# An early place for one set of expert weights, and edge gathers paced by ScalarE, in a graph layer with a routed FFN

## The chip, the cores and the metric

The kernel runs on 1 core of one Trainium2 chip. A core has TensorE (PE, with its weight loads shown apart as PEld), VectorE (DVE), ScalarE (ACT), GpSimd (POOL) and SyncE (SP), each with its own queue of instructions, and 16 DMA engines that all of them share. POOL also issues the indirect DMAs (gathers and scatters by a list of rows). The metric is the time of one execution on the device in microseconds (us); lower is better.

## The reference

Everything is float32. There are N = 6250 nodes of D = 256 features, 100000 edges sorted by their destination, 8 heads, and 8 experts. In outline:

```python
x = x + gnn(layernorm(x), edges, ...)     # graph attention, then a dense FFN
x = x + moe(layernorm(x), ...)            # router, top 2 of 8 experts, FFN of each

# gnn
xn = layer_norm(x, ln1_g, ln1_b)
h = (xn @ W).reshape(N, 8, 32)
e = leaky_relu(a_src[src] + a_dst[dst])           # loops i -> i are added to the edges
alpha = softmax of e over the edges of each dst
agg = segment_sum(h[src] * alpha, dst)
out = layer_norm(agg + xn @ W_res + bias, ln2_g, ln2_b)
return out + gelu_tanh(out @ ffn_w1 + ffn_b1) @ ffn_w2 + ffn_b2     # 256 -> 1024 -> 256

# moe
probs = softmax(x @ Wr + br); top 2, weights scaled to sum 1
y_e = gelu(xe_e @ W1[e] + b1[e]) @ W2[e] + b2[e]                    # 256 -> 1024 -> 256
return sum over the two chosen experts of weight * y_e
```

## The kernel before

The nodes lie in 49 tiles of 128 rows. A first stage (up to about 117 us) makes the tables: `tab_s` in HBM holds each node's `h` and its attention factors, `xt_d` the turned normed input, and the sums `acc_lo` and `acc_hi` in SBUF start with the loops' share.

Then one planned loop (`while s < NG + LASTST ...`, under `tc.manual_schedule()`) writes out the order of all instructions by steps s. It mixes four kinds of work.

- **Edge steps.** There are 196. Step s fetches 512 edges (`fetch`, L865): four gathers of 128 rows of `tab_s` into one `gs` buffer; there are four such buffers. The later stages of an edge step stand in later steps: `spread` (s), `turn_spread` (s+1), `give` (s+2), `weigh` (s+3, DVE: L905 and L909, which frees `gs`), `add_tiles` (s+4, PE L924), and, where a group of steps ends, `add_nodes` (s+5: PE L949, ACT L952 into `added`) and `sum_up` (s+6, DVE L961). There are 110 groups. Edges are taken from the last destinations to the first.
- **Residual products** (`first_unit`, 25 units of two tiles): load of `xt_d` into `xtf`, product with `wres` (L1225), eviction into `rg`, store to `res_d`.
- **Node units** (`node_unit`, 25): when all edges into two tiles are summed, DVE divides and normalises (`divide`, `norm_out`), ACT applies it (`norm_rows`), the dense FFN runs (`net`: `turn` L1025, eight `up` L1042 with eviction to `ht` L1046, `down` L1055), DVE adds up (`add_out`, `take_up`, `norm_new`), and PE makes the router's logits (L1197). Every two units, `chunk_tasks` ranks the tokens (`mark`, `count`, `rank`), makes the list of blocks that are now complete (`enlist`), and scatters the normed rows into `xs` (POOL, L1458), sorted by expert. After the list of the next to last chunk, `clear` (L1474) writes zeros behind each expert's rows, eight DMAs of 390 KB; scatters that stand behind the clears wait until these have landed.
- **Expert blocks** (`block_loads`, `block_unit`; 53 on these inputs): 256 rows of one expert (a few have 128). SP loads W1 and W2 of the expert (1 MB each) and the rows `xb` (L1529); DVE notes the destinations (L1551); then the same `net`; DVE adds the bias (L1561), ACT scales (L1567), and POOL gives the rows back to the output with an adding indirect DMA, two per block (L1571). A block's rows are loaded once the scatters of the chunk that completes it have landed.

Each queue works in order. A step has room for so much work of each engine (`ROOM`: PE 7.5 us, less 1.3 for the edges; POOL one operation besides the gathers). Tasks wait in `pending`, in the order in which they were made, and go into a step when the tasks they need stand in an earlier one; a new unit or block is made only while the queued PE work is under `QUEUE` = 40 us. The last node unit is `urgent`: its tasks go in front.

**Places in SBUF.** `acc_hi` is freed when node tile KHI has been divided (around step 64); only then does the pool `moew` open there, with two sets of expert weights, and only if the pool `first` of the residual products (`wres`, two `xtf`, two `rg`) is closed. A third set (`moew3`) comes when the edges are over. So no expert block stands in the first third of the edge steps.

Of the kernel before, what the change touches and what calls it, by code (L numbers as in the profile page):

```python
# [223 lines left out]
def gnn_moe_kernel(  # L224
# [613 lines left out]
    first_ = ctx.enter_context(ExitStack())  # L838
    fp = first_.enter_context(tc.tile_pool(name="first", bufs=2, side="right"))
    wres = fp.tile([P, KD, D], F32, name="wres", bufs=1)  # L840
# [11 lines left out]

    def step_tiles(s, a):

        q, i = order[s]
        t0, m = groups[q]
        return a[:, t0:t0 + G * m].rearrange("p (j m) -> p j m", m=m)[:, :, i]

    def fetch(s):
        gs = bg.tile([P, G, DT], F32, name="gs")  # L860
        q, i = order[s]
        t0, m = groups[q]
        for j in range(G):
            t = t0 + j * m + i
            nc.gpsimd.indirect_dma_start(  # L865
                out=gs[:, j, :], out_offset=None, in_=tab_s,
                in_offset=bass.IndirectOffsetOnAxis(ap=srce[:, t:t + 1], axis=0))
        live[s, "gs"] = gs
# [16 lines left out]
    def turn_spread(s):  # L885
        po = cps.tile([P, KD, 2 * P], F32, name="pt", bufs=2)
        nc.tensor.transpose(po[:, 0, :P], live[s, "oh"].rearrange("p j r -> p (j r)"), ident)  # L887
        oht = bw.tile([P, P], F32, name="oht")
        nc.scalar.activation(oht, po[:, 0, :P], AF.Copy)
        live[s, "oht"] = oht  # L890

    def give(s):

        pz = bps.tile([P, P], F32, name="pz")[:, :G * 2 * H]
        nc.tensor.matmul(pz, live.pop((s, "oht")), live[order[s][0], "qd"].rearrange(  # L895
            "p j c -> p (j c)"), start=True, stop=True)
        fac = bw.tile([P, G * 2 * H], F32, name="fac")
        nc.scalar.activation(fac, pz, AF.Copy)  # L898
        live[s, "pz"] = fac
# [15 lines left out]
    def add_tiles(s):  # L915

        q, i = order[s]
        last = i == groups[q][1] - 1
        oh, msg = live.pop((s, "oh")), live.pop((s, "msg"))
        if i == 0:  # L920
            live[q, "pl"] = bps.tile([P, DA], F32, name="pl")
        pl = live[q, "pl"]
        for j in range(G):
            nc.tensor.matmul(pl[j * W32:(j + 1) * W32, :], oh[:, j, :], msg[:, j, :],  # L924
                             start=i == 0, stop=last)
        if last:
            part = bw.tile([P, DA], F32, name="part")
            nc.scalar.activation(part, pl, AF.Copy)
            live[q, "part"] = part
# [16 lines left out]
    def add_nodes(q):  # L946
# [3 lines left out]
        added = bw.tile([P, 2, DA], F32, name="added")  # L950
        for b in range(2):
            nc.scalar.activation(added[:, b, :], p2, AF.Copy, scale=here[:, b, q:q + 1])  # L952
# [66 lines left out]
    def turn(src, to, env, scale=None):  # L1019
# [8 lines left out]
        if scale is None:  # L1028
            nc.scalar.activation(xt[:, :, :n * P], pt[:, :, :n * P], AF.Copy)
        else:  # L1030
            for k in range(KD):
                nc.scalar.activation(xt[:, k, :n * P], pt[:, k, :n * P], AF.Identity,  # L1032
                                     bias=scale[:, KD + k:KD + k + 1], scale=scale[:, k:k + 1])
        env[to] = xt

    def up(c, env, w1, func, b):
# [7 lines left out]
        for e in range(c - 1, c + 1) if c % 2 else ():  # L1044
            ht = cw.tile([P, 2 * P], F32, name="ht", bufs=2 * KF)
            nc.scalar.activation(ht[:, :W], ph[:, e % 2, :W], func, bias=b[:, e:e + 1], scale=1.0)  # L1046
            env["ht", e] = ht
# [10 lines left out]
    turns, downs_, ups_ = [], [], []  # L1058
# [3 lines left out]
    def net(env, src, deps, w1, w2, func, b, more=(), scale=None, more2=()):  # L1062
# [5 lines left out]
        ups = [task(lambda c=c: up(c, env, w1(), func, b()), "PE", 0.46 * n, [tn, *more, *free])  # L1068
# [17 lines left out]
        downs_.append(dn[-1])  # L1086
        return dn[-1]
# [49 lines left out]
    def norm_rows(n, env):  # L1137
        for j in range(n):
            oj = env["res"][:, j, :]
            nc.scalar.activation(oj, oj, AF.Identity, bias=env["nm"][:, j:j + 1],  # L1140
                                 scale=env["r"][:, j:j + 1])

    def add_out(n, env):

        o = cw.tile([P, 2, D], F32, name="o", bufs=1)
        nc.vector.tensor_tensor(o[:, :n], env["res"][:, :n],
# [37 lines left out]
    def make_normed(n, env, u):  # L1184
# [3 lines left out]
        for j in range(n):  # L1188
            nc.scalar.activation(xe[:, j, :], env["xin"][:, j, :], AF.Identity,
                                 bias=env["nb"][:, j:j + 1], scale=env["rs"][:, j:j + 1])  # L1190
        env["xe"] = xe

    def logits(n, env):
# [6 lines left out]
        nc.scalar.activation(lt[:, :n * E], pl[:, :n * E], AF.Copy)  # L1200
# [13 lines left out]
    def load_first(t0, n, env):  # L1214
        xt = fp.tile([P, 2, KD, P], F32, name="xtf")
# [13 lines left out]
    def take_product(n, env):  # L1229
        rg = fp.tile([P, 2, D], F32, name="rg")  # L1230
        nc.scalar.activation(rg[:, :n], env["py"][:, :n], AF.Copy)
# [6 lines left out]
    firsts, first_loads = [], []  # L1238

    def first_unit(u):  # L1240
        t0, n, _ = units[u]
        env = {}
        first_loads.append(task(lambda: load_first(t0, n, env), "SP", 0.0,
                                [(d, 0) for d in back(firsts, 2)]))
        pr = task(lambda: first_product(n, env), "PE", 0.95 * n, [(first_loads[-1], 2)], take="py")
        ab = task(lambda: take_product(n, env), "ACT", 0.3 * n,
                  [pr, *[(d, 0) for d in back(firsts, 2)]], free="py")
# [12 lines left out]
    def node_unit(u, env):  # L1260
# [4 lines left out]
        ao = task(lambda: add_out(n, env), "DVE", 0.7 * n, [nr])  # L1265
        dn = net(env, lambda: env["res"], [nr], lambda: w1_sb, lambda: w2_sb,
                 AF.Gelu_apprx_tanh, lambda: prm[:, PR_FB1:PR_FB1 + KF],
                 scale=lambda: prm[:, PR_L2G:PR_L2G + 2 * KD])
        tk = task(lambda: take_up(t0, n, env), "DVE", 0.35 * n, [dn, ao], free="py")
# [60 lines left out]
    def weight(t0, n, env):  # L1330

        nc.scalar.activation(env["less"][:, :n], env["less"][:, :n], AF.Exp)
# [12 lines left out]
    def count(env):  # L1345
# [5 lines left out]
        nc.scalar.activation(rt.rearrange("p a e -> p (a e)"), pr[:, :8 * E], AF.Copy)  # L1351
        env["pr"] = rt

    def rank(t0, n, env):
# [19 lines left out]
        nc.vector.tensor_add(cnt, cnt, incl[:, :, 3])  # L1374

    def enlist(lo, hi, final, begun):
# [32 lines left out]
        if final:  # L1409
# [14 lines left out]
        is_ = cw.tile([P, n * m * E], F32, name="is_", bufs=1).rearrange(  # L1424
            "p (n e) -> p n e", n=n)
        ge = cw.tile([P, n * m * E], F32, name="ge", bufs=1).rearrange(
            "p (n e) -> p n e", n=n)
# [7 lines left out]
        red = cw.tile([P, n], F32, name="redb", bufs=1)  # L1435
# [129 lines left out]
    def weigh_block(env):  # L1565
        for j in range(env["n"]):
            nc.scalar.activation(env["yb"][:, j, :], env["yb"][:, j, :], AF.Copy,  # L1567
                                 scale=env["wt"][:, j:j + 1])
# [11 lines left out]
    def block_loads(i):  # L1580
# [5 lines left out]
        env["pool"] = 1 if len(moew) > 1 and 1 not in pools[-2:] else 0  # L1586
        user = [j for j in range(i) if pools[j] == env["pool"]][-2 + env["pool"]:][:1]
        if env["pool"] == 0 and pools.count(0) < 2:
            user = []
# [48 lines left out]
    with tc.manual_schedule():  # L1638
        nc.sync.dma_start(xs[E * CAP:, :].rearrange("(p r) d -> p r d", r=2),
                          blank[:, None, :].to_broadcast([P, 2, DX]))  # L1640
        while s < NG + LASTST or pending or u < len(units) or len(blocks) < NS:
# [13 lines left out]
            if len(firsts) == len(units) and firsts[-1].step is not None and fp:  # L1655
                first_.close()
                fp = None
            if last_hi and last_hi[0].step is not None and not moew and not fp:
                hi_pool.close()
                moew.append(ctx.enter_context(tc.tile_pool(name="moew", bufs=2, side="right")))  # L1660
            nb = len(blocks) + len(ahead)
            if moew and len(ahead) < 1 + len(moew) and nb < NS and any(n > turn_of[nb]
# [3 lines left out]
            while sum(t.cost for t in pending if t.eng == "PE") < QUEUE:  # L1666
                if (u < len(units) and units[u][2] <= s - LASTST
                        and not (ahead and was_nodes)):
# [15 lines left out]
                elif ahead:  # L1684
# [10 lines left out]
            run_tasks(s, room)  # L1695
            s += 1
# [43 lines left out]
```

## Time and profile before

| | us |
|---|---|
| three runs, median (lowest to highest) | 1735.18 (1732.95 to 1740.66) |
| the profiled execution, its own time | 1738.49 |
| its span, first to last instruction | 1736.7 |
| first gather of the edges starts | 117.5 |
| first product of an expert block starts | 549.7 |
| last gather starts | 1450.2 |
| last product with the dense FFN weights (L1055) starts | 1529.5 |

Mean granted TensorE clock: 0.96 of full speed. DMA moved 334.91 MB.

A group line names line, engine and operation, tile written and tiles read, count; then busy us and the mean ns of one; then the idle time ahead of them and what ended it. In a timeline a row begins with the start and the length, and the bracket at its end has the idle time before it and who released it; rows of the same kind are merged (x4). float32 products are recorded as two matmuls each, and records of neighbours overlap, so that the pace is read from starts and not from the length of one. A wait is put down to what came last.

### The profile page before, as it was taken

To read this page: it belongs to the slowest core of one execution; us is meant where nothing else is said; L and a number is where in the kernel's file an instruction comes from. 1 tells how busy PE (TensorE), PEld (TensorE's weight loads), DVE (VectorE), ACT (ScalarE), POOL (GpSimd) and SP (SyncE) were. 2 spreads that over 40 slices of the span, in tenths; PEclk is the share of its full clock that TensorE was granted. 3 is DMA by queue.
4 is the path that set the end of the run, shared out by engine and by line. 5 is a ranking of instruction groups with operands and counts; after the bars stand their busy time and mean duration, and the time that the engine had idled before them with its cause. 6 is when DMAs were issued, how large, how long until landed. Compare 5 with 4: busy or idle time off the path is not lost.

```text
span 1736.7 us, 28706 instructions
## 1 busy us (share of the span) xinstructions
PE 1555.9 (90%) x8577; PEld 1253.7 (72%) x8577; DVE 982.9 (57%) x3512; ACT 803.7 (46%) x2063; POOL 1155.2 (67%) x1190
## 2 busy tenths in 40 slices
PE   5866898989977999999999999998988998899996
PEld 3643676767656878788888887786866876788885
DVE  6855788888888765766666554337434335131000
ACT  4843454544535554555555444444433433343332
POOL 4437776777777777777778778777777774412222
PEclk9987899999988999999999999999999999999998
DMA  6886564566446667586676676776577766847672
GB/s 199 264 214 203 175 188 141 160 175 164 140 135 219 210 197 211 159 241 167 210 219 195 182 228 199 228 200 208 176 211 211 234 188 196 264 115 233 191 222 41
DMA packets 232898, 334.91 MB, mean 193 GB/s; under 512 B 45169, under 2 KB 189082, under 8 KB 232734
## 3 DMA queue, kind: packets, MB, share of 16 engines
q1 hardware_dynamic: 170892, 190.31, 34.1%
q0 software_dynamic: 58944, 139.58, 30.4%
q10 hardware_dynamic: 2898, 3.09, 0.6%
q8 instruction: 71, 1.16, 0.3%
q14 instruction: 93, 0.76, 0.1%
HBM read 275.95 MB, written 61.10 MB: 194 GB/s over the span
## 4 chain that ended last, share of the span: by engine, by line
PE 48%; DMA 8%; POOL 7%; issue 6%; DVE 5%; ACT 2%; SPq 1%; DVEq 0%; POOLq 0%; ACTq 0%
PE py L1055 20%; PE ph L1042 19%; DMA gs<-tab_s,srce 6%; POOL gs L865 5%; PE pl L924 3%; PE pt L949 1%; PE pt L1025 1%; PE pt L887 1%; DMA out_dram<-yb,tos 1%; ACT turned_in L1032 1%; POOL out_dram L1571 1%; DVE msg L909 1%; PE pz L895 1%; POOL xs L1458 1%; PE ph L1197 1%
## 5 line engine op out<-in xcount | busy, mean ns | idle before, releaser
L865 POOL DMA_INDIRECT gs<-tab_s,srce x784 | 823.3, 1050 | 252.8 <-issue 198.3
L1042 PE MATMUL ph<-turned_in,w1b 128*128 128x256 f32 (+1 forms) x1696 | 422.1, 379 | 8.8 <-ACT turned_in L1032 7.7
L1055 PE MATMUL py<-w2b,ht 128*128 128x256 f32 x1648 | 418.3, 383 | 3.3 <-DMA w2b<-in_L_ffn_W_dram 2.9
L1042 PEld LDWEIGHTS ph<-turned_in,w1b 128*128 128x128 f32 x1696 | 318.7, 194 | 55.2 <-ACT turned_in L1032 12.0
L1055 PEld LDWEIGHTS py<-w2b,ht 128*128 128x128 f32 x1648 | 313.4, 193 | 45.4 <-issue 3.7
L1046 ACT ACTIVATE ht<-ph,pc 128x256 f32<-128x256 f32 (+1 forms) x424 | 175.2, 465 | 363.7 <-PE ph L1042 363.4
L1571 POOL DMA_INDIRECT out_dram<-yb,tos x103 | 166.1, 1613 | 193.4 <-ACT yb L1567 131.7
L909 DVE TENSOR_TENSOR msg<-gs,msg 128x1024 f32<-128x1024 f32 x196 | 240.5, 1227 | 7.0 <-DVE msg L908 0.4
L924 PE MATMUL pl<-msg,oh 128*32 128x264 f32 x1568 | 134.1, 415 | 86.9 <-DVE msg L909 86.5
L905 DVE TENSOR_TENSOR ww<-gs,fac 128x64 f32<-128x64 f32 x196 | 43.8, 224 | 277.9 <-DMA gs<-tab_s,srce 239.2
L1042 PE MATMUL ph<-turned_in,w_sb 128*128 128x256 f32 (+1 forms) x800 | 193.7, 382 | 6.0 <-ACT ht L1046 5.1
L1055 PE MATMUL py<-w_sb,ht 128*128 128x256 f32 x784 | 190.2, 380 | 0.0
L1042 PEld LDWEIGHTS ph<-turned_in,w_sb 128*128 128x128 f32 x800 | 150.1, 194 | 27.6 <-ACT ht L1046 6.5
L1055 PEld LDWEIGHTS py<-w_sb,ht 128*128 128x128 f32 x784 | 144.5, 190 | 25.0 <-issue 3.5
L1458 POOL DMA_INDIRECT xs<-xe,slot x98 | 107.5, 1096 | 55.8 <-issue 41.2
L1046 ACT ACTIVATE ht<-ph,prm 128x256 f32<-128x256 f32 (+1 forms) x200 | 82.6, 467 | 121.5 <-PE ph L1042 121.4
L898 ACT ACTIVATE fac<-pz 128x64 f32<-128x64 f32 x196 | 44.0, 225 | 188.5 <-PE pz L895 105.1
L1561 DVE TENSOR_TENSOR yb<-py,b2b 128x512 f32<-128x512 f32 (+1 forms) x53 | 35.7, 673 | 153.6 <-PE py L1055 153.6
L924 PEld LDWEIGHTS pl<-msg,oh 128*32 128x32 f32 x1568 | 32.1, 110 | 102.8 <-issue 54.4
L952 ACT ACTIVATE added<-pt,here 128x264 f32<-128x264 f32 x220 | 93.8, 478 | 20.1 <-PE pt L949 13.0
L887 PEld LDWEIGHTS pt<-ident,oh 128*128 128x128 f32 x196 | 28.3, 144 | 95.9 <-issue 42.0
L961 DVE TENSOR_TENSOR acc_lo<-acc_lo,added 128x528 f32 x56 | 39.6, 708 | 92.7 <-ACT added L952 79.6
(359 smaller groups left out, 2038.1 us busy)
## 6 DMA issues: line engine op xcount, KB each, us to landing
w1b<-in_L_ffn_W_dram SPq DMA_DIRECT2D x53, 1024.0 KB
w2b<-in_L_ffn_W_dram SPq DMA_DIRECT2D x53, 1024.0 KB
xb<-xs SPq DMA_DIRECT2D x50, 260.0 KB
gs<-tab_s,srce POOLq DMA_INDIRECT x784
b2b<-in_L_ffn_b_dram SPq DMA_DIRECT2D x53, 128.0 KB
tab_s<-hg SPq DMA_DIRECT2D x12, 544.0 KB
xt_d<-xt SPq DMA_DIRECT2D x12, 512.0 KB
xtf<-xt_d SPq DMA_DIRECT2D x24, 256.0 KB
```

The source lines that it names most:

```text
L865: nc.gpsimd.indirect_dma_start(out=gs[:, j, :], out_offset=None, in_=tab_s, in_offset=bass.IndirectOffsetOnAxis(ap=srce[:, t:t + 1], axis=0))
L887: nc.tensor.transpose(po[:, 0, :P], live[s, "oh"].rearrange("p j r -> p (j r)"), ident)
L898: nc.scalar.activation(fac, pz, AF.Copy)
L905: nc.vector.tensor_tensor(ww, gs[:, :, D:], live.pop((s, "pz")).rearrange("p (j c) -> p j c", j=G), op=ALU.mult)
L909: nc.vector.tensor_tensor(msg[:, :, :D].rearrange("p t (h d) -> p t h d", h=H), gs[:, :, :D].rearrange("p t (h d) -> p t h d", h=H), msg[: ...
L924: nc.tensor.matmul(pl[j * W32:(j + 1) * W32, :], oh[:, j, :], msg[:, j, :], start=i == 0, stop=last)
L952: nc.scalar.activation(added[:, b, :], p2, AF.Copy, scale=here[:, b, q:q + 1])
L1042: nc.tensor.matmul(ph[:, c % 2, :W], w1[:, k, c * P:(c + 1) * P], env["in"][:, k, :W], start=k == 0, stop=k == KD - 1)
L1046: nc.scalar.activation(ht[:, :W], ph[:, e % 2, :W], func, bias=b[:, e:e + 1], scale=1.0)
L1055: nc.tensor.matmul(env["py"][:, j, :], env["ht", c][:, j * P:(j + 1) * P], w2[:, c, :], start=c == 0 and "row" not in env, stop=c == KF - 1)
L1458: st = nc.gpsimd.indirect_dma_start(out=xs, out_offset=bass.IndirectOffsetOnAxis(ap=slots[k][:n, t:t + 1], axis=0), in_=xes[u // 2][:n, pl ...
L1571: st = nc.gpsimd.indirect_dma_start(out=out, out_offset=bass.IndirectOffsetOnAxis(ap=tos[:, b, j:j + 1], axis=0), in_=env["yb"][:, j, :], ...
```

## The change

1. **A place for one weight set beside the edges.** The pool `first` goes. A pool `moew1` (`ew0`), opened ahead of the edges, holds one set (W1, W2). Until the residual products are through, its W2 space holds `wres` and three `rg`, its W1 space four `xtf`; so loads of the residual inputs run four units ahead and not two. Once the last residual unit is stored, the set serves the expert blocks. `moew2` (one set) opens when `acc_hi` is free, `moew3` after the edges, as before: three sets in the end as before, but the first one earlier. While there is one set, a block unit is made only when its weights and rows are on their way, and nodes and blocks needn't take turns. A block takes the set that was used longest ago.
2. **Space for it**: `added` has one buffer and not two; `ht` 12 and not 16, with dependencies that keep the ups behind the downs that free their buffers; `add_out` multiplies in place in `res` and therefore stands behind the turn that reads `res`; the tiles of `enlist` are sized once.
3. **Gathers behind ScalarE.** All of ScalarE's operations of a step are noted (`act`). The second, third and fourth gather of step s wait for the operation at one, two and three quarters of step s-1's list, if that has at least eight.

```diff
-    first_ = ctx.enter_context(ExitStack())
-    fp = first_.enter_context(tc.tile_pool(name="first", bufs=2, side="right"))
-    wres = fp.tile([P, KD, D], F32, name="wres", bufs=1)
+    ew0 = gnn.enter_context(tc.tile_pool(name="moew1", bufs=1))
+    early = ew0.tile([P, KD, F], F32, name="w1b").rearrange("p k (i c) -> p (k i) c", c=2 * D)
+    early2 = ew0.tile([P, KF, D], F32, name="w2b")
+    wres = early2[:, :KD, :]
+    early = [early[:, i, :] for i in range(4)] + [
+        early2[:, i * KD:(i + 1) * KD, :].rearrange("p k d -> p (k d)") for i in range(1, 4)]
...
+    acts = [[]]
+    def act(*a, **k):
+        i = nc.scalar.activation(*a, **k)
+        acts[-1].append(i.ins)
+        return i
...
+        ahead_ = acts[-2] if len(acts) > 1 else []
         for j in range(G):
             t = t0 + j * m + i
-            nc.gpsimd.indirect_dma_start(
+            ld = nc.gpsimd.indirect_dma_start(
                 out=gs[:, j, :], out_offset=None, in_=tab_s,
                 in_offset=bass.IndirectOffsetOnAxis(ap=srce[:, t:t + 1], axis=0))
+            if j and len(ahead_) >= 2 * G:
+                tc.add_manual_dep(ld.ins, ahead_[len(ahead_) * j // G].name, ...)
...
-        added = bw.tile([P, 2, DA], F32, name="added")
+        added = bw.tile([P, 2, DA], F32, name="added", bufs=1)
...
-            ht = cw.tile([P, 2 * P], F32, name="ht", bufs=2 * KF)
+            ht = cw.tile([P, 2 * P], F32, name="ht", bufs=3 * KF // 2)
...
+        last = dns[-1][-KF // 2:] if dns else []
+        ups = [task(lambda c=c: up(c, env, w1(), func, b()), "PE", 0.46 * n,
+                    [tn, *more, *free, *[(d, 0) for d in last[:max(0, (c + 1) // 2 - KF // 4)]]])
...
-        o = cw.tile([P, 2, D], F32, name="o", bufs=1)
+        o = env["res"]
...
         first_loads.append(task(lambda: load_first(t0, n, env), "SP", 0.0,
-                                [(d, 0) for d in back(firsts, 2)]))
+                                [(d, 0) for d in back(products, 4)]))
...
-        ao = task(lambda: add_out(n, env), "DVE", 0.7 * n, [nr])
+        ao = task(lambda: add_out(n, env), "DVE", 0.7 * n, [turns[-1]])
...
-        env["pool"] = 1 if len(moew) > 1 and 1 not in pools[-2:] else 0
-        user = [j for j in range(i) if pools[j] == env["pool"]][-2 + env["pool"]:][:1]
+        used = [max((j for j in range(i) if pools[j] == p), default=-1) for p in range(len(moew))]
+        env["pool"] = used.index(min(used))
+        user = [j for j in used if j == min(used) and j >= 0]
...
-            if last_hi and last_hi[0].step is not None and not moew and not fp:
+            if len(firsts) == len(units) and firsts[-1].step is not None and not moew:
+                moew.append(ew0)
+            if last_hi and last_hi[0].step is not None and len(moew) == 1:
                 hi_pool.close()
-                moew.append(ctx.enter_context(tc.tile_pool(name="moew", bufs=2, side="right")))
+                moew.append(ctx.enter_context(tc.tile_pool(name="moew2", bufs=1, side="right")))
...
-            if moew and len(ahead) < 1 + len(moew) and nb < NS and any(n > turn_of[nb]
+            if len(ahead) < len(moew) and nb < NS and any(n > turn_of[nb]
...
-                        and not (ahead and was_nodes)):
+                        and not (ahead and was_nodes and len(moew) > 1)):
...
-                elif ahead:
+                elif ahead and (len(moew) > 1 or all(ahead[0][1][t].step is not None
+                                                     for t in ("lw", "lx"))):
...
             run_tasks(s, room)
+            acts.append([])
             s += 1
```

Every `nc.scalar.activation` of the loop becomes `act`, with the same arguments.

## The prediction

> **What bounds the kernel now.** I read the page first (busy shares, the 40 slices, the groups), then a table of windows by stage, then the waits of the stage 1060 to 1450 us, then the timeline of the stretch around the last edge gather.
>
> ```profile
> PE 1555.9 (90%) x8577; PEld 1253.7 (72%) x8577; DVE 982.9 (57%) x3512; ACT 803.7 (46%) x2063; POOL 1155.2 (67%) x1190
> ...
> PE   5866898989977999999999999998988998899996
> ...
> POOL 4437776777777777777778778777777774412222
> ...
> L865 POOL DMA_INDIRECT gs<-tab_s,srce x784 | 823.3, 1050 | 252.8 <-issue 198.3
> ...
> L1571 POOL DMA_INDIRECT out_dram<-yb,tos x103 | 166.1, 1613 | 193.4 <-ACT yb L1567 131.7
> ```
>
> ```profile
> 300.00:556.00 256.00, 215.30 (x1235) 165.41 (x1234) 217.24 (x801) 130.35 (x341) 195.19 (x219) 0.93 0.57 168
> 556.00:1060.00 504.00, 497.89 (x2879) 409.38 (x2878) 328.35 (x1152) 261.89 (x650) 397.01 (x397) 1.00 0.67 199
> 1060.00:1450.00 390.00, 360.22 (x2041) 292.59 (x2040) 169.63 (x526) 157.07 (x407) 307.47 (x278) 0.97 0.70 207
> 1450.00:1500.00 50.00, 41.88 (x183) 33.47 (x182) 18.49 (x81) 13.13 (x31) 19.21 (x23) 0.90 0.84 249
> 1500.00:1737.00 237.00, 215.22 (x1078) 187.93 (x1076) 33.15 (x149) 85.45 (x204) 53.66 (x38) 0.98 0.58 165
> ```
>
> ```profile
> DVE ww L905 <- DMA gs<-tab_s,srce: 187.8, 41, 9.2
> ```
>
> ```profile
> 417.72 3.46 PE py L1055 x16
> ```
>
> The windows give, in order, the busy time of PE, its weight loads, DVE, ACT and POOL, then clock, DMA share and GB/s. A gather costs POOL 1.05 + 0.30 us (the issue gap), a give-back 1.61 + 0.30. Four gathers and one such operation make about 7.1 us, the pace of a step. From 150 to 1450 us I find only 23 us of POOL gaps longer than 0.5 us: **POOL sets when the edges end** (the last gather starts at 1450.18). TensorE is full from 556 to 1060, idles 41 us in 300:556 and 30 us in 1060:1450 (behind gathers), and after 1450 has only expert blocks. So the end is the last gather plus what TensorE still has to do. Sixteen matmul records take 3.46 us: one 128x128x256 product (two records) costs 0.432 us. The groups of ups, downs and residual products hold 5124 records, 128 of them half wide, so 2530 products.
>
> **The change, part by part.**
>
> *Blocks before the edges end.* The built order of both programs shows how many products stand ahead of the last edge step: 1970 of 2530 before, 2080 after. They fall into steps 1 to 67 (about 117 to 556 us). There TensorE idled 34 us (117:300) and 41 us (300:556) and had a clock of 0.87 and 0.93. So 110 x 0.432 = 47.5 us fits into what was idle. At the last gather 550 products remained before, 448 remain after: **-44.1 us** of tail.
>
> *Six give-backs move with them*: 64 stood ahead of the last gather, now 70. On the queue that sets the end of the edges this is 6 x 1.91 = **+11.5 us**.
>
> *The first dry spell.* In the changed order block 37's last downs stand in steps 196 and 197; then PE has only edge sums until block 38. Blocks 38 to 41 need the rows of the next to last chunk, and these wait behind the list, the eight clears of L1474, and the scatters. Before, blocks 35 to 37 covered this chain:
>
> ```profile
> 1459.92 0.17 DVE L1449 CAST endi<-start 128x8 int32<-128x8 f32 x1
> ```
>
> ```profile
> 1462.33 11.15 SPq L1474 DMA_DIRECT2D xs<-blank  x8
> ...
> 1491.96 0.37 SPq L1529 DMA_DIRECT2D xb<-xs  x1
> ```
>
> ```profile
> 1450.18 0.95 POOL L865 DMA_INDIRECT gs<-tab_s,srce  x1 [0.30 <-issue]
> ...
> 1479.62 0.96 POOL L1458 DMA_INDIRECT xs<-xe,slot  x1 [21.43 <-issue]
> ```
>
> ```profile
> 1496.92 0.17 DVE L1551 COPY tos<-xb 128x2 int32<-128x2 int32 x1 [11.06 <-DMA xb<-xs]
> ```
>
> From the list (1459.9) to the rows in SBUF (1496.9) is 37 us; the turn and its eviction add 1.4 (1482.72 to 1484.05). The list is now made one step earlier, about 3 us behind the last gather instead of 9.9, so block 38 starts about 41 us behind it. Less 3 us of edge sums: **+38 us** of idle TensorE (bounds 27 and 44: the list up to 11 us earlier; more weight loads in front of the rows).
>
> *The second dry spell.* The last node unit is now made in step 206, not 202, because three waiting blocks fill the planner's 40 us of queued work. Block 41's last three downs stand right behind the turn for its logits, and the next product is block 42's. In the trace of before this chain costs: turn and eviction 1.0, logits 1.2, choose and mark 1.6, exp with its table load and the counts 2.0, DVE up to the list 10.9 (1553.19 to 1564.05), SP 2.0, the rows 4.6 (1566.07 to 1570.64), the turn 1.9; 25 us, less 2.6 of downs. Block 42's second weights now stand behind three first ones and three sets of rows: about 2 us more. **+25 us** (bounds 18 and 35). Before, blocks 39 to 41 stood in between and the rows came 3.4 us ahead of their turn.
>
> *Clock after a stall.*
>
> ```profile
> 1488.11 2.05 PE L1055 MATMUL py<-w2b,ht 128*128 128x256 f32 x4 [2.91 <-DMA w2b<-in_L_ffn_W_dram]
> 1489.95 1.91 PE L1042 MATMUL ph<-turned_in,w1b 128*128 128x256 f32 x4
> 1491.66 1.87 PE L1055 MATMUL py<-w2b,ht 128*128 128x256 f32 x4
> ```
>
> After 2.9 us of idling, three groups of four need 5.25 us instead of 2.59: 2.7 us lost. Two dry spells: **+5.4**. What before loses there itself goes: stalls 3.0 + 0.2 + 1.3 + 0.7 + 2.9 and slow groups 4.5: **-12.6**.
>
> The Trainium skill, "TensorE: Matmul & The Clock Gate", section "Why this matters for your kernels", speaks against the change here: a gap of about 3 us already puts the array back to half its clock. Its window of 3.4 us at half rate would make 1.7 us per spell, 3.4 in all instead of 5.4, and the total 2 us less.
>
> *One `added` buffer (L952), 12 `ht`, `o` in place.* ScalarE's next `added` now waits until DVE has added the one before. Set side by side from the two engines' timelines, DVE is later than that in 27 of the first 66 groups, by 77 us in sum. Behind this wait on ScalarE stand the step's `ht` and `turned_in`, and PE waits for those. Bounds: nothing (ScalarE is busy 130 of 256 us) and 77. The `ht` ring just fits the one-to-one order of ups and downs: nothing. `add_out` behind the turn costs DVE no instruction, and block work covers it; without that cover, one step per unit.
>
> *One weight set early.* W1 of the next block is issued when the last up of this one stands, its first up two steps later (13 us). The w2b issued at 1479.83 landed 8.1 us later, so it is hidden; without that slack some 5 us for each of five blocks. Residual inputs run four ahead on SP, which bounds nothing.
>
> *Gathers wait for ScalarE.* Gathers 2 to 4 of step s wait for operations at 1/4, 1/2 and 3/4 of step s-1. Queued behind them on POOL are the step's scatter or give-back and the next gathers; DVE's L905 and the block rows wait for those. Where POOL is behind (1060:1450) DVE is three steps further, so the wait is long over: 0. Where TensorE is behind, gathers land 12 to 25 us before L905 needs them; the wait takes some 2 us of that. Bounds: 0 and 20 us, one lost lead when POOL becomes the bound. Gains are bounded too: the 299 gathers that overlap DVE's L909 took 1.18 us, the other 485 took 0.97, in all 70 us of excess, which a better spacing could shrink.
>
> I take +3 us for the last three together (from -20, all old POOL gaps gone, to +35), since before already had the pace of POOL in this stage.
>
> **Sum.** Last gather: +11.5 + 3 = +14.5. Tail: -44.1 + 38 + 25 + 5.4 - 12.6 = +11.7. Together +26 us. The profiled execution took 1738.5 us (span 1736.7) and would take 1764.5; it lay 3.3 us over the median of 1735.2, so I predict **1761 us**.
>
> **Rivals.**
>
> *Faster: the gathers stop setting the pace.* If the spacing takes away at least half of the 70 us of overlap, POOL no longer limits 1060:1450 and TensorE keeps its 30 us there; it then also arrives at the last gather with about 15 us of products left, which shorten the first spell. 1761 - 30 - 15 = **1716 us**. For it: the two gather durations. Against: POOL has no gaps there, so a wait that is already over moves no gather. It decides from a mean gather of 1.00 us downwards.
>
> *Slower still: the early steps stretch.* The one `added` buffer and the four blocks now standing in 300:556, where DVE was busy 217 of 256 us, make TensorE and ScalarE wait for DVE; POOL then idles at its four `gs` buffers. Half of the 77 us is lost: **1797 us**.
>
> *A wash.* The lists come earlier, or the change finds its room without loss: first spell 27, second 18, edges +0: 1761 - 11 - 7 - 11 = **1732 us**, within half a per cent of before.
>
> **How the numbers follow.** Forecast 0.62, faster rival 0.13, slower rival 0.13, wash 0.12. The forecast's own bounds give 1743 to 1785. For 8 in 10 the range takes in the wash and the lower part of the slower rival: 1732 to 1790. A measurement can tell about 0.5%, 8.7 us. Faster: 0.14; same: 0.13 (the wash and the forecast's lower end); slower: 0.73.
>
> **What would show it.** Right: the last gather at about 1465 us; more products per window from 300 to 556 with the clock near 1.0; two holes in PE's slices behind the last gather, some 38 and 25 us, ended by a block's rows; each with matmuls at half clock behind it; a last node unit that starts later. Wrong: gathers whose mean falls to 1.00, a last gather before 1440, POOL gaps behind ScalarE in the steady stage, or PE busy through the lists.

## The result, and the profile after

The changed kernel takes **1779.21 us** (median of four runs, 1773.55 to 1782.41) against 1734.74 us for the kernel before: ratio 1.0241, 95% interval 1.0219 to 1.0262. It is slower, as forecast, by 44 us where the forecast had 26. Ratios, here and below, leave out runs over 1.5% above the fastest of the same kernel, so they need not be the quotient of the medians. The profiled execution has a span of 1780.5 us, so 43.8 more than before's 1736.7.

The page after (busy shares, slices, groups), the lines that answer to those shown of before:

```profile
PE 1560.5 (88%) x8577; PEld 1258.6 (71%) x8577; DVE 981.2 (55%) x3512; ACT 810.0 (45%) x2071; POOL 1162.2 (65%) x1190
...
PE   4857898879999999999999989998998995685996
...
POOL 4437755677777878787887877877777776220222
...
L877 POOL DMA_INDIRECT gs<-tab_s,srce x784 | 830.7, 1060 | 275.5 <-issue 158.5
...
L1592 POOL DMA_INDIRECT out_dram<-yb,tos x103 | 168.7, 1637 | 226.9 <-ACT yb L860 190.8
```

The engines do hardly more work than before; the span has grown by idle time. A gather still takes 1.06 us (before 1.05). Two holes have come into TensorE's row near its end (`56` in the slices around 1513 us, `5` around 1625), and POOL's row is thinner in its sixth to eighth slice, 223 to 356 us (`556`; `767` before).

The last gather starts at 1491.28 (before 1450.18). So 41.1 us are lost ahead of it and 2.7 behind it. Windows of both kernels between the same edge steps (first gather, the gathers of step 66 and of step 114, last gather, end) show where. First before, then after:

```profile
117.50:530.00 412.50, 344.79 (x1987) 261.36 (x1987) 323.16 (x1137) 201.57 (x538) 313.58 (x330) 0.91 0.57 168
530.00:876.70 346.70, 335.07 (x1914) 274.55 (x1913) 238.34 (x847) 180.63 (x446) 270.37 (x276) 0.99 0.67 198
876.70:1450.20 573.50, 542.39 (x3093) 442.69 (x3092) 280.35 (x915) 250.89 (x639) 453.40 (x421) 0.98 0.70 206
1450.20:1736.70 286.50, 256.90 (x1258) 221.22 (x1256) 51.62 (x230) 98.59 (x234) 72.85 (x60) 0.96 0.63 180
```

```profile
118.10:566.10 448.00, 389.33 (x2173) 301.69 (x2174) 328.29 (x1153) 222.45 (x577) 319.24 (x333) 0.92 0.60 179
566.10:923.10 357.00, 351.34 (x2033) 287.81 (x2032) 236.66 (x852) 191.02 (x472) 283.87 (x279) 1.00 0.67 194
923.10:1491.30 568.20, 531.60 (x3000) 432.97 (x2998) 283.64 (x934) 238.20 (x613) 450.57 (x420) 0.96 0.69 198
1491.30:1780.50 289.20, 214.41 (x1045) 184.35 (x1045) 43.41 (x190) 86.60 (x203) 64.31 (x54) 0.87 0.55 159
```

After each window stand its length and the busy time of PE, its weight loads, DVE, ACT and POOL. In the first 66 steps TensorE has 44.5 us more to do (389.3 against 344.8), and they take 35.5 us longer: its idle time there fell only from 67.7 to 58.7 us. The next 48 steps take 10.3 us longer, with TensorE almost full in both. The last 82, at the pace of POOL, take 5.3 us less. Behind the last gather TensorE has 42.5 us less to do and 45.2 us more idle time.

A finer table of the first 64 steps comes from the timeline of TensorE, cut at each step's `pz` product (L895, after L911; "0 to 17" runs from the `pz` of step 0 to that of step 18), with the products (residual, ups, downs; two records each) that stand between the cuts in the trace, and the idle time in front of TensorE's rows. The last column is a run told of below.

| steps | before: us, products, idle | after | order alone |
|---|---|---|---|
| 0 to 17 | 106.4, 88, 28.8 | 115.7, 120, 24.6 | 116.7, 120, 24.1 |
| 18 to 37 | 136.7, 184, 10.8 | 147.3, 170, 20.6 | 143.8, 170, 17.1 |
| 38 to 63 | 166.3, 178, 26.6 | 187.7, 264, 13.0 | 185.2, 264, 12.6 |

The 104 more products are 44.9 us at 0.432 each; the time grew by 41.3 and the idle time shrank by 8.0. Only in steps 38 to 63, where 86 more products stand, was much of the idle time used. In steps 0 to 17, too, products now stand in six steps that had none, yet the idle time fell by just 4.2: there DVE waits longer until gathers have landed. Before (117.2 to 223.6 us), then after (118.1 to 233.8):

```profile
DVE ww L905 <- DMA gs<-tab_s,srce: 22.0, 7, 4.6
```

```profile
DVE ww L921 <- DMA gs<-tab_s,srce: 30.7, 6, 10.4
```

The DMA engines move 222 GB/s in this stretch, 185 before. That the residual inputs, now loaded four units ahead, delay the gathers fits these rows, but no run shows it. In steps 18 to 37 there are 14 products fewer, but TensorE's idle time is 9.8 us longer and its granted clock 0.92, before 0.98. The gathers of step 18 still start at 214.8 (before 215.5), those of step 38 at 367.9 (before 341.5): here TensorE's delay reaches POOL.

### The profile page after: what moved, and what is told of

It reads as the page before. It is cut to its first block, busy times and chain, and to the rows that moved or that the text cites. A ratio compares the mean times of both kernels' runs of the same rounds, so it can differ in the third digit from the quotient of the medians.

```text
span 1780.5 us, 28947 instructions
## 1 busy us (share of the span) xinstructions
PE 1560.5 (88%) x8577; PEld 1258.6 (71%) x8577; DVE 981.2 (55%) x3512; ACT 810.0 (45%) x2071; POOL 1162.2 (65%) x1190
## 4 chain that ended last, share of the span: by engine, by line
PE 54%; DVE 13%; DMA 12%; POOL 8%; issue 7%; ACT 4%; SPq 1%; DVEq 1%; ACTq 0%; POOLq 0%
PE ph L1058 21%; PE py L1071 20%; DMA gs<-tab_s,srce 8%; POOL gs L877 5%; PE pl L940 4%; DVE msg L925 2%; PE pt L965 2%; PE pt L1041 2%; PE pt L903 2%; PE py L1244 1%; DVE bnst L482 1%; ACT turned_in L860 1%; PE pz L911 1%; POOL r L625 1%; DMA out_dram<-yb,tos 1%
## 5 line engine op out<-in xcount | busy, mean ns | idle before, releaser
L921 DVE TENSOR_TENSOR ww<-gs,fac 128x64 f32<-128x64 f32 x196 | 43.8, 224 | 318.2 <-DMA gs<-tab_s,srce 280.6
L1058 PE MATMUL ph<-turned_in,w_sb 128*128 128x256 f32 (+1 forms) x800 | 197.3, 384 | 11.9 <-ACT counts L860 6.9
L1071 PE MATMUL py<-w_sb,ht 128*128 128x256 f32 x784 | 194.3, 384 | 0.0
L860 ACT ACTIVATE added<-pt,here 128x264 f32<-128x264 f32 x220 | 93.7, 477 | 73.5 <-DVE acc_hi L977 55.9
L903 PEld LDWEIGHTS pt<-ident,oh 128*128 128x128 f32 x196 | 27.8, 142 | 95.5 <-issue 42.5
L860 ACT ACTIVATE oht<-pt 128x128 f32<-128x128 f32 x196 | 55.1, 281 | 57.8 <-PE pt L903 46.8
```

The lines of the kernel that those rows point to most:

```text
L860: i = nc.scalar.activation(*a, **k)
L921: nc.vector.tensor_tensor(ww, gs[:, :, D:], live.pop((s, "pz")).rearrange("p (j c) -> p j c", j=G), op=ALU.mult)
L1058: nc.tensor.matmul(ph[:, c % 2, :W], w1[:, k, c * P:(c + 1) * P], env["in"][:, k, :W], start=k == 0, stop=k == KD - 1)
L1071: nc.tensor.matmul(env["py"][:, j, :], env["ht", c][:, j * P:(j + 1) * P], w2[:, c, :], start=c == 0 and "row" not in env, stop=c == KF - 1)
```

## The experiments

Three theories of the 41 us ahead of the last gather were to be told apart. A: the gathers' waits for ScalarE take POOL's lead. B: the one `added` buffer ties ScalarE, and TensorE behind it, to DVE. C: the new order itself. The trace after speaks for each: the profile puts 55 us ahead of gathers down to ScalarE's operations (before: none; 23 us of it in waits over 0.5 us, the rest little more than the 0.3 us between any two gathers), ScalarE waits for L977 by 55.9 us (before: none), and the work has moved.

The runs with before at 1733 us stand in one part below; the others met three chips on which the kernel before takes 1995 to 2002 us. Each ratio is to before on the run's own chip.

### Where before takes 1733 us

**The change again, and its order alone.** The second kernel is the changed one without the gathers' waits and with two `added` buffers. For the second buffer alone there is no room (21.2 KB per partition where 20.4 are left), so the router's turned rows, `turned_rt`, get one buffer in place of two:

```diff
-            if j and len(ahead_) >= 2 * G:
-                tc.add_manual_dep(ld.ins, ahead_[len(ahead_) * j // G].name, ...)
...
-        added = bw.tile([P, 2, DA], F32, name="added", bufs=1)
+        added = bw.tile([P, 2, DA], F32, name="added")
...
-        xt = cw.tile([P, KD, 2 * P], F32, name=f"turned_{to}")
+        xt = cw.tile([P, KD, 2 * P], F32, name=f"turned_{to}", bufs=1 if to == "rt" else 2)
```

> The changed kernel itself, unchanged, beside a fresh run of the kernel before on the same chip. If before is near 1735 again, 1779 (ratio 1.024). If before is near 2000, the runs so far give two readings. What they add up to, if the parts are independent: order and places (with one `added` buffer) 1.010 to 1.019 without the waits, times the waits' 0.961 to 0.970, so 0.97 to 0.99, near the 0.980 of the version with two `added` buffers. What the prediction's steps say, whose terms hold for any chip: slower than before, 1.015 to 1.024.

> The changed kernel with two `added` buffers and without the gathers' waits: what is left of the change is the early place, the order that follows from it, 12 `ht`, and the multiplication in place. With before at 1735: if the order alone carries the 41 us (theory C: TensorE's 44.5 us of more work in the first 66 steps went into only 9 us of its idle time), 1770 to 1780; if the waits or the buffer carry it (A, B), about 1742. With before near 2000: 2030 if the `added` buffer is worth nothing, as before with one buffer (ratio 1.002) says; below 2010 if it matters in the new order.

Measured: the changed kernel 1777.57 us, ratio 1.0247 (1.0230 to 1.0264); its order alone 1779.87 us, ratio 1.0257 (1.0233 to 1.0282). So the waits and the buffer together cost nothing: A and B both fall, and the last gather of the order alone still starts at 1487.98. The single `turned_rt` buffer hides no gain: ScalarE's one wait ahead of `turned_rt` is 3.1 us, 3.2 in the changed kernel, for the product that it copies. That the waits gain just what the buffer costs, this run alone does not exclude. The group of `added`, after and then with the order alone (busy, mean ns, idle time ahead and its releaser):

```profile
L860 ACT ACTIVATE added<-pt,here 128x264 f32<-128x264 f32 x220 | 93.7, 477 | 73.5 <-DVE acc_hi L977 55.9
```

```profile
L860 ACT ACTIVATE added<-pt,here 128x264 f32<-128x264 f32 x220 | 93.7, 477 | 17.1 <-PE pt L961 9.4
```

And the waits of POOL's gathers in steps 18 to 37 (us, times, longest), in the same order:

```profile
POOL gs L877 <- DVE msg L925: 19.2, 7, 5.2
POOL gs L877 <- issue: 13.8, 45, 0.6
POOL gs L877 <- ACT oht L860: 12.9, 5, 5.0
POOL gs L877 <- ACT ht L860: 5.4, 9, 1.1
POOL gs L877 <- ACT added L860: 3.7, 2, 2.8
```

```profile
POOL gs L877 <- DVE msg L921: 33.4, 10, 5.7
POOL gs L877 <- issue: 19.9, 66, 0.3
```

The 55.9 us of waits are gone and nothing is faster: they lay in ScalarE's idle time. Without its waits for ScalarE, POOL waits as long (53.3 us in these rows against 55.0), now for a free `gs` buffer, which `msg` frees. What the profile names as releaser was not what set the pace. TensorE's own waits there have grown (before, then after):

```profile
PE pl L924 <- DVE msg L909: 3.8, 3, 2.5
PE py L1223 <- ACT rg L1231: 2.9, 2, 1.4
```

```profile
PE py L1242 <- ACT w2b L860: 6.9, 4, 2.4
PE ph L1058 <- ACT counts L860: 5.6, 1, 5.6
PE py L1069 <- ACT w2b L860: 5.1, 1, 5.1
```

(`w2b` is here the early place, used as `rg`.) TensorE waits 12.0 us for evictions of residual products, 2.9 before; with the order alone it is 7.0. That the new places of the residual products are the cause was only argued from these rows; the run for it, `g2` below, does not bear it out.

**The end mended.** Scatters ahead of the clears, and no block that needs the next to last chunk ahead of the last node unit:

```diff
-            cleared.extend([task(lambda e=e: clear(e), "SP", 0.0, [li]) for e in range(E)])
+            cleared.extend([task(lambda e=e: clear(e), "SP", 0.0, [li, *[(d, 3) for d in sc]])
+                            for e in range(E)])
...
-                elif ahead and (len(moew) > 1 or all(ahead[0][1][t].step is not None
+                elif ahead and not (u == len(units) - 1 == ahead[0][1]["units"]) and (
+                        len(moew) > 1 or all(ahead[0][1][t].step is not None
```

> The changed kernel with the end of its order mended in two places: the scatters of the next to last chunk stand ahead of the eight clears (they write rows ahead of those that are cleared, so they needn't wait for them), and no block that needs the next to last chunk is made before the last node unit. Part 1's early place, part 3's waits and the early steps are untouched. If the two dry spells are what the change costs behind the last gather, as the prediction has it (38 + 25 + 5.4 us there; 34 and 23 us read from the trace after), the rows of block 38 come about 16 us earlier, the node unit's FFN (64 half-wide products, some 14 us) stands in the first spell, and blocks 38 to 41 cover the second: the stretch from the last gather to the end shrinks by 45 to 55 us against the changed kernel's on the same chip (289 us where that took 1779). If rows or weights are late for another reason (the DMA queues), each spell stays as long as it was, and the time within 10 us of the changed kernel's.

Measured: 1742.28 us, ratio 1.0044 (1.0020 to 1.0068): 35.3 us less than the changed kernel beside it, and still 9.0 more than before. The last gather starts where it did (1492.78), the stretch behind it takes 250.9 us and not 289.2. First the first spell of the changed kernel in the timeline, from the last downs ahead to block 38's turn; then the second, from the last logits to the turn of block 42 and the ups behind it:

```profile
1487.92 1.13 PE L1071 MATMUL py<-w2b,ht 128*128 128x256 f32 x4
...
1494.37 11.72 SPq L1495 DMA_DIRECT2D xs<-blank  x8
...
1495.46 1.10 PE L940 MATMUL pl<-msg,oh 128*32 128x264 f32 x8 [6.41 <-DVE msg L925]
...
1497.82 1.10 PE L940 MATMUL pl<-msg,oh 128*32 128x264 f32 x8 [1.25 <-DVE msg L925]
...
1510.81 0.96 POOL L1479 DMA_INDIRECT xs<-xe,slot  x1 [10.79 <-DMA xs<-blank]
...
1523.39 2.69 SPq L1550 DMA_DIRECT2D xb<-xs  x3
...
1527.12 1.97 PE L1041 MATMUL pt<-ident,xb 128*128 128x128 f32 x8 [26.44 <-DMA xb<-xs]
```

```profile
1596.77 0.51 PE L1216 MATMUL ph<-wr_sb,turned_rt 128*128 128x8 f32 x4
...
1613.06 0.38 SPq L1550 DMA_DIRECT2D xb<-xs  x1
...
1618.52 1.11 PE L1041 MATMUL pt<-ident,xb 128*128 128x128 f32 x4 [18.77 <-DMA xb<-xs]
...
1622.79 11.33 PE L1058 MATMUL ph<-turned_in,w1b 128*128 128x256 f32 x40
...
1633.96 1.89 PE L1071 MATMUL py<-w2b,ht 128*128 128x256 f32 x8
```

With the end mended, the first spell's stretch reads:

```profile
1495.43 1.62 SPq L1535 DMA_DIRECT2D w1b<-in_L_ffn_W_dram  x2
...
1498.64 1.49 POOL L1479 DMA_INDIRECT xs<-xe,slot  x1 [0.30 <-issue]
...
1508.27 0.69 PE L1041 MATMUL pt<-ident,res 128*128 128x128 f32 x2 [6.09 <-ACT res L860]
...
1517.53 1.11 PE L1041 MATMUL pt<-ident,xb 128*128 128x128 f32 x4 [8.57 <-DMA xb<-xs]
...
1518.44 5.78 PE L1058 MATMUL ph<-turned_in,w_sb 128*128 128x128 f32 x32
```

The scatters no longer wait for the clears. Block 38's turn stands 24.8 us behind the last gather and not 35.8, so 11 us earlier and not 16: four weight loads of 1 MB are issued ahead of the rows. The second spell is gone (no idle time over 1.1 us from 1518 to the end). But the node unit's 32 ups stand behind that turn in TensorE's queue and did not fill the first spell. So the stretch shrank by 38.3 us of 45 to 55 expected, with the same 1045 records of TensorE behind the last gather: most of the 45.2 us of idle time that the tail gained were these two spells.

### Where before takes 1995 to 2002 us

**The parts one by one.** The changed kernel without its waits (the first hunk above), twice; the kernel before with part 3 alone (first hunk below; every `nc.scalar.activation` of the loop becomes `act`), twice; the kernel before with one `added` buffer (second hunk below); the changed kernel with two (the other two hunks above).

```diff
-            nc.gpsimd.indirect_dma_start(
+            ld = nc.gpsimd.indirect_dma_start(
...
+            if j and len(ahead_) >= 2 * G:
+                tc.add_manual_dep(ld.ins, ahead_[len(ahead_) * j // G].name, ...)
...
-        added = bw.tile([P, 2, DA], F32, name="added")
+        added = bw.tile([P, 2, DA], F32, name="added", bufs=1)
```

> The changed kernel without its part 3: the second to fourth gather of a step no longer wait for ScalarE; the order of all instructions stays that of the changed kernel. In the changed kernel the gathers fall behind those of before by 36 us between about 208 and 566 us (step 17 to step 66), and by some 5 to 10 us more in the steady stage. Theory A (the waits carry it: gathers are now released by ScalarE's operations of the step ahead, and POOL cannot run ahead into its four gs buffers): the last gather goes from 1491 back to about 1455, the time from 1779 to about 1742. Theory B (the one `added` buffer couples ScalarE, and behind it TensorE, to DVE): unchanged, 1775 to 1782, and ScalarE still waits some 56 us for L977. Theory C (the new order itself, more block and residual products in early steps): unchanged, 1775 to 1782.

> The changed kernel without its part 3 once more, beside a fresh run of the kernel before. The first run of it was made where the kernel before took 2002 us: there ScalarE and TensorE stood idle for up to 14 us at a time for nothing that the profile shows, and this kernel took 1.019 of before. If the kernel before is at about 1735: theory A (the waits carry the 41 us by which the last gather comes later) 1742, last gather at about 1455; theory C (the new order of the early steps carries it, as the 1.019 of the first run says) 1770 to 1780, last gather at 1480 to 1491. If before is near 2000 again: about 2030 by both.

> The kernel before with part 3 alone: its second to fourth gathers wait for ScalarE's operations at 1/4, 1/2 and 3/4 of the step ahead; order, buffers and places as before. Theory A: the last gather moves from 1450 to about 1485, the time from 1735 to about 1770. Theories B and C: 1735, within 6 us. The forecast's own term for this part was 0 to 20 us with about 2 taken.

> The kernel before with part 3 alone once more. In its first run, where before took 2002 us, it was faster: 0.9705. If before is at about 1735: theory A 1770 (the waits cost what POOL's lead was worth); theory C within 6 us of 1735; and if what the first run showed holds here too (paced gathers leave the other queues' transfers and the engines' instructions more room), 1715 to 1730. If before is near 2000 again: about 1930.

> The kernel before with one `added` buffer in place of two, nothing else; the order of instructions is the same. Theory B: ScalarE waits some 50 us for L977 in all, most of it at 200 to 550 us, and the time goes from 1735 to about 1765. Theories A and C: the waits on L977 may show, but the time stays at 1735 within 6 us, because ScalarE's idle time takes them up.

> The changed kernel with two `added` buffers again (the room comes from the turned rows of the router, `turned_rt`, which get one buffer in place of two); the order of instructions is the same. With before at 1735: theory B (ScalarE's 56 us of waits for L977 hold TensorE up) about 1745; theory A (the gathers' waits) 1770 to 1782; theory C (the new order) 1775 to 1782. The waits of `added` for L977 go in any case.

| kernel | median us | ratio to before (95%) | last gather |
|---|---|---|---|
| changed, no waits | 2030.55; again 2032.68 | 1.0191 (1.0102 to 1.0280); 1.0104 (0.9989 to 1.0218) | 1732.9; 1725.9 |
| before, waits added | 1932.53; again 1925.80 | 0.9705 (0.9618 to 0.9792); 0.9607 (0.9544 to 0.9670) | 1631.3; 1643.3 |
| before, one `added` | 2000.81 | 1.0018 (0.9961 to 1.0075) | 1670.4 |
| changed, two `added` | 1962.16 | 0.9801 (0.9733 to 0.9869) | 1665.6 |

The first run of each pair and the third row were on one chip, the second runs and the last row on another. Here too one `added` buffer costs nothing in the kernel before, and the order without the waits is slower than before in the first run; in the second the interval takes in 1. But the waits gain 3 to 4% in the kernel before, and the changed kernel with them (and two `added` buffers) takes 1962 us where the one without them (and with one) takes 2033: it is faster than before here. The waits of ScalarE for causes that the trace cannot place (remote, issue), for the kernel before with one `added` buffer and with the waits added:

```profile
ACT part L928 <- remote: 79.7, 19, 13.2
ACT ht L1046 <- remote: 70.8, 19, 11.8
ACT fac L898 <- remote: 51.1, 16, 13.4
ACT oht L889 <- remote: 48.0, 21, 6.2
```

```profile
ACT ht L856 <- remote: 61.2, 18, 8.4
ACT part L856 <- remote: 58.4, 13, 13.1
...
ACT fac L856 <- remote: 40.0, 9, 14.8
```

The first has 262 us of remote waits over 0.9 us, the two runs of the second 203 and 231. Over all nine runs on these chips the sums are 262 to 305 us without the gathers' waits (four runs) and 196 to 278 with them (five); where before takes 1733 us no kernel has one.

**The end mended further, and other starts.** The first kernel is the one with the mended end, with the turn of a block that needs the next to last chunk one step later; the second has the old pace of the residual units besides; the third is the kernel before with the mended end.

```diff
-        dn = net(env, lambda: env["xb"], [(env["lx"], 2), env["lp"]], lambda: env["w1"],
+        dn = net(env, lambda: env["xb"],
+                 [(env["lx"], 3 if env["units"] == len(units) - 1 else 2), env["lp"]], ...
...
-                                [(d, 0) for d in back(products, 4)]))
+                                [(d, 0) for d in back(firsts, 2)]))
...
-                  [pr, *[(d, 0) for d in back(firsts, 3)]], free="py")
+                  [pr, *[(d, 0) for d in back(firsts, 2)]], free="py")
```

> The changed kernel with its end mended as in the run before (1742), and one thing more: the turn of a block that needs the next to last chunk comes one step later, so that in PE's queue the last node unit's ups stand ahead of it. In the run before, 32 half-wide ups (5.8 us) waited behind a turn that stood idle for 8.6 us until its rows came. If TensorE's order is what was left of the first spell, the time falls by 5 to 8 us, to 1735; if the rows' 4 MB of weights ahead of them set it, the products only change places and it stays at 1742.

> The same with the residual units at the pace of before again: their loads run two units ahead, not four. By the built order steps 0 to 37 then hold just the products of before (78 and 184; the changed kernel has 110 and 174), the early place serves blocks from about step 50 on, and 46 products more than before stand ahead of the last edge step, not 110. If what the edges lost by step 38 (28 us behind before, where no block product stands yet) comes from the residual products' new places, the last gather comes 20 us or more earlier than in the changed kernel (1491), at 1460 to 1468, against some 28 us of products that move behind it; the time lands at 1725 to 1740. If each moved product costs the edges its own time wherever it goes (110 products, 41 us), the last gather is at 1467 and the time 1735 to 1745. If the prediction's step held (early products go into idle time), the last gather is at 1452 and the time near 1720.

> The kernel before with the same mending of its end (scatters ahead of the clears, blocks of the next to last chunk behind the last node unit, their turn a step later). Its own losses behind the last gather are stalls of 8.1 us and 4.5 us of slow groups, so at most 12.6 us can go: 1721 to 1735. If the mended end is worth nothing where blocks 35 to 37 cover the chain anyway, 1733 within 4 us.

These three ran on the third of these chips. Measured: g1 1920.97 us, ratio 0.9673 (0.9577 to 0.9769); g2 1943.89, 0.9756 (0.9669 to 0.9842); g3 2006.09, 1.0026 (0.9967 to 1.0085). The stretch behind the last gather takes 253.9 us in g1 and 296.7 in the changed kernel with two `added` buffers on the second: 42.8 less, where the first mending gave 38.3 beside the changed kernel. That the later turn is worth the difference is not shown across chips. In g3 the mended end is worth nothing, as expected if before's blocks 35 to 37 cover the chain anyway.

g2 speaks against the residual products as the cause of the slower start: its gather of step 64 comes at 616.8 and g1's at 617.2, though 64 products fewer stand ahead of the last edge step. Its stretch behind the last gather is 22.8 us longer (276.7), and its last gather is at 1678.7 against 1664.6. The expectation was in times of a chip on which before takes 1733 us (its products are counted by the planner's steps, one step off the cuts of the table above), and g2 met 278 us of remote waits of ScalarE and g1 196, so this settles only that the old residual pace gains nothing visible here.

## Why the prediction was right in direction and 18 us short

- *POOL sets when the edges end.* From step 114 on, yes: POOL idles for no stretch over 0.5 us there, and 568.2 against 573.5 us. In the first 66 steps, no: POOL lost 48.6 us in such stretches (14.9 before), about half of it waiting for `gs` buffers that `msg` had yet to free.
- *Blocks before the edges end, -44.1.* Right behind the last gather: 213 records fewer, 106 products, 46.0 us. **The step that failed is the other half of the sentence, that 47.5 us "fits into what was idle".** The 66 first steps have 44.5 us more work and 35.5 us more time. This term stood at 0 for the last gather and measured +35.5, with 10.3 more up to step 114, where TensorE is full, and 5.3 less behind it. The idle time was read as a sum over 117 to 556 us; but products are issued in the planned order and fill a wait only where they stand in front of it (with the end mended, 32 ups whose input was ready stood behind a turn that waited 8.6 us for its rows). In steps 38 to 63 idle time went from 26.6 to 13.0; in steps 0 to 17 it fell by just 4.2, behind gathers that landed later; in steps 18 to 37 it grew. Nor did the clock come near 1.0 from 300 to 556 us: 0.94, with 1278 records where 1235 were.
- *Six give-backs, +11.5.* They came (70 ahead of the last gather, 64 before), but four of them in the first 66 steps, where POOL had idle time, and three more in the next 48, where TensorE is the bound. In the stretch that POOL sets there are 44, before 45. Measured: nothing.
- *First dry spell, +38.* 26.4 us for the rows, 6.4 and 1.3 in front of the edge sums: 34.1. Chain and releaser as forecast: clears, scatters, rows.
- *Second dry spell, +25.* 18.8 + 1.8 + 2.3 = 22.9, with the last node unit's divide at 1529.3 (before 1469.2).
- *Clock after a stall, 2.7 each.* By starts, the 40 records behind the second spell take 11.2 us (1622.79 to 1633.96); 20 products at 0.432 are 8.64: 2.5 us lost. Behind the first spell, where the turn stands in the slow time too, the ups lost 1.7. The window of 3.4 us at half rate that the Trainium skill gives ("TensorE: Matmul & The Clock Gate", section "What's actually happening") makes 1.7 by estimate. But the records stand at half pace for 5.1 us behind the second spell (1622.79 to 1627.85), so the window is short here, and the row was the better price for that spell.
- *The tail in sum, +11.7.* Measured +2.7: 46.0 us of products are gone, but only 42.5 us of busy time (3.5 are slow records), and the idle time grew by 45.2. So idle and slow time grew by 48.7 us, not 55.8.
- *One `added` buffer, gathers behind ScalarE: +3 together.* Nothing, by the run with the order alone. The wait came (55.9 us, within the bound of 77 read from the two engines' timelines), but it was no price.
- *The rivals.* The faster one is out: a gather's mean is 1.06 us. (Its 70 us of overlap are 63 by its own means: 299 gathers at 1.18 for 0.97.) The one that is slower still named the right place, the early steps, for the wrong reason: half of the 77 us through `added`. The run without these waits is as slow. The wash is out with the edges at +41; its shorter spells (27 and 18) were half right at 34.1 and 22.9.
- *The total.* That it is only 18 us off is luck in part: the edges were 26.6 us too low (14.5 for 41.1), and the tail 9.0 too high (11.7 for 2.7).

What stays open is which part of the new order slows steps 18 to 37, that hold 14 products fewer than before and take 10.6 us longer, and whether the residual loads slow the steps ahead of them. The order-alone run still has 12 `ht`, `o` in place and the residual inputs in the early place.

## What to carry to other kernels

Work that is moved into the idle time of an engine with a fixed order can cost most of its own length there (here 35.5 of 44.5 us): look for the very step and wait that are idle, and for what ends that wait; a sum of idle time over a stage is no room. Covering work that is taken from the end of a program can leave each chain behind it as a hole, so list the chains (here clears, scatters, rows; and logits, list, rows) and shorten them in the same change. A long list of new waits is no price: take them away, and see whether the time moves.

## What the runs showed of the hardware that was not expected

The same program, on the same inputs, takes 1733 to 1735 us in some of these runs and 1995 to 2002 us on three other chips. There ScalarE waits 196 to 305 us, over all kernels that were run, for something that the profile calls remote (up to 15.0 us at a time; none where before takes 1733 us), while a gather takes no longer (1.00 to 1.03 us against 1.05) and the same bytes are moved. With gathers held back to ScalarE's pace there are mostly fewer such waits (196 to 278 us against 262 to 305), and the kernel before gets 3 to 4% faster by the holding back. That it gets faster through these waits is not shown, and what they are the profile does not show. Where before takes 1733 us, the changed kernel is no slower with the gathers held back and one `added` buffer than without and with two; the kernel before with held gathers was not run there. So a change can have opposite signs on two chips: the changed kernel is 2.4% slower on the one, and with two `added` buffers 2.0% faster on another.
